# The gates, B and C of each mixer group as 2x2 block products with seven multiplications, and work moved from POOL to ACT

## The chip, the cores and the metric

The kernel runs on one core of one Trainium2 chip. The metric is device time in microseconds (us), the median of several runs. All tensors are float32.

## The reference

A perceiver layer on 8 x 64 = 512 tokens of width 512: cross attention to 8 x 1601 context tokens, then a mixer of the Mamba-2 kind, then a routed low-rank feed-forward. Only the mixer is touched:

```python
proj = jnp.einsum('bld,pd->blp', hidden_states, in_proj_w)   # layernormed x
gate = proj[..., :I]
hbc = proj[..., I:I + CONV_DIM]
dt = proj[..., -H:]
pad = jnp.pad(hbc, ((0, 0), (K - 1, 0), (0, 0)))
conv = conv_bias
for k in range(K):                                            # K = 4 taps
    conv = conv + pad[:, k:k + L, :] * conv_weight[:, k]
xBC = jax.nn.silu(conv)                                       # x, B and C
...                                                           # scan over L = 64 steps
y = y + x * D
yn = y * rsqrt(mean(y * y over the group) + EPS) * norm_weight * silu(gate)
out = jnp.einsum('bli,di->bld', yn, out_proj_w)
```

There are 64 heads of 64 channels, so I = 4096, in 8 groups of 512 channels; each group has a B and a C of 128 channels.

## The kernel before

Cross attention takes the first 2.3 ms and the mixer most of the last 0.5 ms. The Tile framework orders the instructions of each engine's queue from the program order, its own costs and the free buffers; an engine then runs its queue strictly in order. `with tc.issue_after(ins):` adds a constraint to that: instructions of the block that run on the engine of `ins` are queued after `ins`.

The mixer (`mixer_and_routed`) works group by group, channels on partitions, all 512 tokens as columns. A group has ten weight tiles of 512 x 128: n = 0 to 3 the gate, 4 to 7 x, 8 B, 9 C. `project` multiplies one of them with `mx_xnT` in four steps over the width into one PSUM bank with tag `pj` (three of them, shared with `project_out`, whose tile is called `mo`). In the trace each float32 matmul shows as two MATMUL instructions, so a tile is x8. A gate tile goes through Silu on ACT (L1122) into `sg`. An x, B or C tile is convolved on VectorE (DVE): one TENSOR_SCALAR for the first tap and the bias (L1127) and three SCALAR_TENSOR_TENSOR (STT) for the other taps (L1133), all four reading PSUM; then Silu on ACT (L1138) into `xbc`.

The work is pipelined over two groups. In the first half of a group's iteration PE projects tiles 8, 9 and 4 to 7 of group g, with `mix`, `scan` and `gate` of the group before (`old`) between them; GpSimd (POOL) multiplies x by D in `skip` (L1145) into `y`. Then ACT loads the table of Ln and Exp, and takes the decays of the next group (`decay`, L1104 and L1109) and the norm of the old one (`norm`, L1211 to L1215). In the second half PE alternates the four gate tiles with the four `project_out` of the old group (mo0 to mo3); DVE adds each to `x` with the norm's factor `rs` (L1228), which frees its bank. Group 0 has no old group; the last group has no next one and runs its own mix and scan between its gates. After it comes the tail: the last output product and the routed feed-forward.

`load_out` scales the output weights by the norm's weights on POOL (L1015). POOL also forms the decays' inputs `av` (L1089) and adds up the squares (L1196, L1198).

The cross attention's projections already use a 2x2 block product with seven multiplications. The plan and the sums of weights:

```python
FIRST = (("a", "L11", "R11"), ("d", "S2", "T2"), ("b", "S1", "T1"), ("c", "S3", "T3"))
SECOND = (("a", "L12", "R21"), ("b", "S4", "R22"), ("c", "L22", "T4"))
# weight_sums, on POOL: S1 = L21 + L22, S2 = S1 - L11, S3 = L11 - L21, S4 = L12 - S2
```

In the queries' stage (`project_queries`) these products have 256 columns (L204); their results are put together by one ACT copy and five adds on DVE per pair (L220 to L233).

Of the kernel before, what the change touches and what calls it, by code (L numbers as in the profile page):

```python
# [9 lines left out]
F32 = mybir.dt.float32  # L10
AF = mybir.ActivationFunctionType  # L11
# [950 lines left out]
def mixer_and_routed(ctx, tc, c, x, done, w_in, w_out, w_ra, b_w, out):  # L962
# [18 lines left out]
    def bank(tag, shape, name, bufs=1):  # L981
        return (ps4 if tag in ("pj", "y1") else ps).tile(shape, F32, tag=tag, name=name, bufs=bufs)
# [23 lines left out]
    def load_out(G):  # L1006

        g = G.g
        G.wo = wst.tile([P, GC, D], F32, tag="w_out", name=f"w_out_{g}")
        nc.sync.dma_start(  # L1010
            out=G.wo, in_=w_out[g * GC * P : (g + 1) * GC * P, :].rearrange("(n p) o -> p n o", p=P)
        )
        for n in range(GC):
            ct = g * GC + n
            nc.gpsimd.tensor_scalar(G.wo[:, n, :], G.wo[:, n, :], c.nw[:, ct : ct + 1], None, op0=ALU.mult)  # L1015

# [4 lines left out]
    for tt in range(NTT):  # L1021
# [11 lines left out]
    dt = big.tile([P, NTT, H2], F32, name="dt")  # L1033
    z = big.tile([P, NTT, H2], F32, name="sp_z")
    nc.vector.tensor_tensor(z, pdt, c.dtb.unsqueeze(1).to_broadcast([P, NTT, H2]), ALU.add)
    e = big.tile([P, NTT, H2], F32, name="sp_e")

    nc.vector.tensor_scalar(dt, z, 0.0, None, op0=ALU.max)
    nc.vector.scalar_tensor_tensor(out=e, in0=dt, scalar=-2.0, in1=z, op0=ALU.mult, op1=ALU.add)
    nc.scalar.activation(e, e, AF.Exp)  # L1040
    u = big.tile([P, NTT, H2], F32, name="sp_u")
    nc.vector.tensor_scalar(u, e, 1.0, None, op0=ALU.add)
    lu = big.tile([P, NTT, H2], F32, name="sp_lu")
    nc.scalar.activation(lu, u, AF.Ln)
# [9 lines left out]
    nc.scalar.activation(a_sb, c.a_log, AF.Exp)  # L1054
    a = big.tile([P, NTT, H2], F32, name="a")
    nc.vector.scalar_tensor_tensor(
        out=a, in0=dt, scalar=-1.0, in1=a_sb.unsqueeze(1).to_broadcast([P, NTT, H2]),
        op0=ALU.mult, op1=ALU.mult,
    )


# [21 lines left out]
    def steps(G, tt):  # L1083


        if tt == 0:
            G.av, G.dec = [], grpp.tile([P, NTT, HPG, S], F32, tag="dec", name="dec")
        av = wk.tile([P, 2, HH, S], F32, tag="av", name="av", bufs=4)
        nc.gpsimd.tensor_tensor(  # L1089
            av,  # L1090
            ah[:, :, tt, G.g, :].unsqueeze(3).to_broadcast([P, 2, HH, S]),
            c.upto1.unsqueeze(1).unsqueeze(1).to_broadcast([P, 2, HH, S]),
            ALU.mult,
        )
        G.av.append(av)
# [16 lines left out]
    def project(G, n):  # L1112

        pj = bank("pj", [P, NT], "pj", 3)
        for dc in range(DC):
            nc.tensor.matmul(  # L1116
                pj, lhsT=G.w[:, dc, n, :], rhs=xnT[:, dc, :], start=dc == 0, stop=dc == DC - 1
            )
        if n < GC:
            if n == 0:  # L1120
                G.sg = grpp.tile([P, GC, NT], F32, tag="sg", name="sg")
            return nc.scalar.activation(G.sg[:, n, :], pj, AF.Silu).ins  # L1122
        if n == 8:
            G.xbc = grpp.tile([P, GC + 2, NT], F32, tag="xbc", name="xbc")
        ct = G.g * GC + n - GC if n < 8 else (I2 // P + G.g if n == 8 else I2 // P + G2 + G.g)
        acc = wk.tile([P, NT], F32, tag="acc", name="acc", bufs=3)
# [5 lines left out]
        for k in range(1, KC):  # L1132
# [4 lines left out]
            )  # L1137
        return nc.scalar.activation(G.xbc[:, n - GC, :], acc, AF.Silu).ins  # L1138

    def skip(G):  # L1140

        G.y = grpp.tile([P, GC, NT], F32, tag="y", name="y")
        for n in range(GC):
            ct = G.g * GC + n
            nc.gpsimd.tensor_scalar(G.y[:, n, :], G.xbc[:, n, :], c.dk[:, ct : ct + 1], None, op0=ALU.mult)  # L1145

# [74 lines left out]
    def project_out(G, tt):  # L1221
        po = bank("pj", [P, D], "mo", 3)
        for n in range(GC):
            nc.tensor.matmul(  # L1224
                po, lhsT=G.y[:, n, tt * P : (tt + 1) * P], rhs=G.wo[:, n, :],
                start=n == 0, stop=n == GC - 1,
            )
        nc.vector.scalar_tensor_tensor(  # L1228
            out=x[:, tt, :], in0=po, scalar=G.rs[tt], in1=x[:, tt, :], op0=ALU.mult, op1=ALU.add
        )  # L1230


    w = big.tile([P, DC, E + E * R], F32, name="w_ra")
    bw = big.tile([P, D], F32, name="bw")

# [5 lines left out]
    def load_routed():  # L1241
        nc.sync.dma_start(out=w, in_=w_ra.rearrange("(dc p) o -> p dc o", p=P))
        nc.sync.dma_start(out=bw, in_=b_w)

    def route(tt):
        xnT = wk.tile([P, DC, P], F32, tag="xnT", name="rt_xnT")
        layernorm_T(nc, c, small, ps, x, tt, xnT, tag="px", bufs=2, pbufs=1, copy=nc.scalar.copy)
# [13 lines left out]
        nc.vector.tensor_scalar(rw, rank, first, top, op0=ALU.is_equal, op1=ALU.mult)  # L1261
        wh = wk.tile([P, E, R], F32, tag="wh", name="wh")
        nc.vector.tensor_tensor(
# [6 lines left out]
        nc.tensor.transpose(pt, wh.rearrange("p e r -> p (e r)"), c.ident)  # L1270
        whT = wk.tile([P, P], F32, tag="whT", name="whT")
        nc.scalar.copy(whT, pt)
        po = bank("y1", [P, D], "ro")
        nc.tensor.matmul(po, lhsT=whT, rhs=bw, start=True, stop=True)
        o = wk.tile([P, D], F32, tag="o", name="o")
        nc.vector.tensor_tensor(o, x[:, tt, :], po, ALU.add)
        nc.sync.dma_start(out=out[tt * P : (tt + 1) * P, :], in_=o)


    g0 = groups[0]  # L1280
    for tt in range(NTT):
        steps(g0, tt)
    last = None
    for tt in range(NTT):
        last = decay(g0, tt)
    for g in range(G2):
# [10 lines left out]
        with tc.issue_after(last):  # L1297

            for n, behind in (
                (None, ((mix, 0),)),  # L1300
# [6 lines left out]
            ):  # L1307
                if n is not None:
                    silus.append(project(G, n))
                if old:  # L1310
                    for what, tt in behind:
                        what(old, tt)
            skip(G)
        with tc.issue_after(silus[-1]):
            table = load_ln_exp(nc).ins
        with tc.issue_after(table):
            if new:
                decay(new, 0)
                decay(new, 1)
        gates = [lambda n=n: project(G, n) for n in range(GC)]  # L1320
        if new:
# [3 lines left out]
        if old:  # L1325
            with tc.issue_after(table):
                last = norm(old, range(NTT))
        with tc.issue_after(last):
            for n in range(GC):
                if not new and n == NTT - 1:  # L1330
                    scan(G, n)
                    squares(G, n)
                last_gate = gates[n]()
                if not new:

                    for tt in ((0, 1), (2,), (3,), ())[n]:
                        mix(G, tt)
                    if 0 < n < NTT - 1:
                        scan(G, n - 1)
                        squares(G, n - 1)  # L1340
                    if n == 2:
                        scan(G, n)
                        squares(G, n)
                if old:
                    project_out(old, n)
        last = last_gate

    G = groups[-1]
    with tc.issue_after(last):
        table = load_ln_exp(nc).ins  # L1350
# [75 lines left out]
```

## Time and profile before

| | us |
|---|---|
| median of 3 runs (lowest, highest) | 2804.25 (2802.63, 2805.12) |
| the profiled execution | 2806.07 |
| its span, first to last instruction | 2804.4 |
| mixer, first projection to last gate | 2308.2 to 2767.4 |
| groups 1 to 6, from the start of one to the next | 58.8 to 59.6 |

In the profile, PE is TensorE's matmuls, PEld its weight loads, DVE VectorE, ACT ScalarE, POOL GpSimd, and SP the queue that issues DMAs. A line of the timeline has start, duration, engine, source line, operation, output<-inputs, shapes and count; in brackets the engine's idle time before it and what ended it. Matmul ends are modelled, so PE's pace is read from start to start; DVE instructions overlap a little in the same way.

### The profile page before, as it was taken

What the parts mean: (1) busy time and instruction counts of PE and PEld (TensorE: products, weight loads), DVE (VectorE), ACT (ScalarE), POOL (GpSimd) and SP (SyncE); (2) the same over time, 40 slices, a digit from 0 to 9 for tenths busy, and PEclk for the clock granted to TensorE, in tenths of its full rate; (3) what the DMA queues carried; (4) which work ended last, traced back from release to release, by engine and by line L of the source; (5) the groups of instructions that cost most, each with busy time, mean ns of one, the idle gap of its engine ahead of it and who ended that gap; (6) DMA issues with size and microseconds to landing.
All of it is one profiled execution on the core that took longest, in us unless ns stands there. A gap on an engine that the chain in (4) does not pass through costs nothing.

```text
span 2804.4 us, 38363 instructions
## 1 busy us (share of the span) xinstructions
PE 2777.7 (99%) x14972; PEld 1980.5 (71%) x14972; DVE 1717.9 (61%) x3044; ACT 726.3 (26%) x1314; POOL 837.4 (30%) x786
## 2 busy tenths in 40 slices
PE   9899999999999999999999999999999999999998
PEld 7677777777777777877777777778777554444444
DVE  4556676566666666765766676667656326444554
ACT  3322223222222322232222222222322103222222
POOL 4313323322222332233222223322322214333431
PEclk9999999999999999999999999999999999999999
DMA  4821322131223213221311232132212541112200
GB/s 156 276 90 46 88 67 55 53 103 44 48 54 90 54 45 89 67 55 52 103 45 48 54 89 54 48 85 67 61 31 80 168 140 38 53 53 86 72 16 15
DMA packets 277230, 206.02 MB, mean 73 GB/s; under 512 B 155676, under 2 KB 240538, under 8 KB 276026
## 3 DMA queue, kind: packets, MB, share of 16 engines
q1 hardware_dynamic: 277050, 203.57, 25.5%
q8 instruction: 119, 1.95, 0.3%
q14 instruction: 61, 0.50, 0.1%
HBM read 180.87 MB, written 22.66 MB: 73 GB/s over the span
## 4 chain that ended last, share of the span: by engine, by line
PE 87%; DVE 3%; ACT 1%; DMA 1%; issue 0%; POOL 0%; SPq 0%; ACTq 0%; DVEq 0%
PE pav L596 13%; PE psc L526 12%; PE pj L1116 8%; PE pv_a L445 6%; PE pv_b L445 6%; PE pk_b L385 6%; PE pv_c L445 6%; PE pk_c L385 6%; PE pk_a L385 5%; PE mo L1224 4%; PE pv_d L445 3%; PE pk_d L385 3%; PE psn L414 2%; DVE acc L1133 1%; PE pvl L468 1%; PE po_d L741 1%
## 5 line engine op out<-in xcount | busy, mean ns | idle before, releaser
L531 DVE SCALAR_TENSOR_TENSOR attn<-psc,rk,mask_sb 128x256 f32<-128x256 f32 (+1 forms) x832 | 364.4, 475 | 190.6 <-PE psc L526 188.8
L580 POOL TENSOR_TENSOR sm<-attn 128x512 f32<-128x512 f32 x64 | 82.0, 1281 | 1196.0 <-ACT attn L578 1196.0
L596 PE MATMUL pav<-attn,v 128*128 128x256 f32 (+1 forms) x1664 | 384.3, 381 | 0.0
L526 PE MATMUL psc<-q,kT 128*128 128x256 f32 x1536 | 367.5, 380 | 0.0
L596 PEld LDWEIGHTS pav<-attn,v 128*128 128x128 f32 (+1 forms) x1664 | 311.1, 190 | 55.4 <-issue 11.1
L583 POOL TENSOR_TENSOR sm<-sm,attn 128x512 f32<-128x512 f32 x256 | 339.9, 1328 | 28.9 <-DVE attn L574 10.6
L526 PEld LDWEIGHTS psc<-q,kT 128*128 128x128 f32 x1536 | 287.5, 190 | 77.1 <-issue 29.9
L1116 PE MATMUL pj<-mx_xnT,w_in 128*128 128x512 f32 x640 | 296.3, 603 | 1.3 <-DVE acc L1133 1.3
L574 DVE TENSOR_TENSOR attn<-attn,nb 128x1024 f32<-128x1024 f32 x192 | 224.7, 1215 | 58.1 <-ACT nb L571 57.3
L445 PEld LDWEIGHTS pv_a<-wv,cx 128*128 128x128 f32 x1536 | 196.0, 191 | 48.2 <-issue 41.4
L578 ACT ACTIVATE attn<-attn 128x1024 f32<-128x1024 f32 x192 | 203.4, 1059 | 79.8 <-DVE attn L574 77.2
L445 PE MATMUL pv_a<-wv,cx 128*128 128x128 f32 x1536 | 213.8, 279 | 0.0
L542 DVE TENSOR_TENSOR mx<-mx,attn 128x512 f32<-128x512 f32 x256 | 212.3, 829 | 2.0
L1116 PEld LDWEIGHTS pj<-mx_xnT,w_in 128*128 128x128 f32 x640 | 115.2, 190 | 129.4 <-issue 124.7
L385 PE MATMUL pk_a<-cx,wk 128*128 128x417 f32 (+1 forms) x512 | 193.3, 500 | 0.8 <-ACT qrs L110 0.8
L396 ACT ACTIVATE ksq<-kT 128x834 f32<-128x834 f32 (+1 forms) x128 | 109.2, 871 | 145.9 <-DVE kT L377 145.9
L385 PEld LDWEIGHTS pk_a<-cx,wk 128*128 128x128 f32 x512 | 97.2, 190 | 46.1 <-issue 20.8
L1228 DVE SCALAR_TENSOR_TENSOR x<-mo,rs,x 128x512 f32<-128x512 f32 x32 | 24.0, 750 | 165.1 <-PE mo L1224 110.4
L1224 PE MATMUL mo<-w_out,y 128*128 128x512 f32 x256 | 118.1, 597 | 0.0
L643 POOL TENSOR_TENSOR o<-o,f 128x512 f32<-128x512 f32 x31 | 40.0, 1291 | 232.7 <-DMA f<-sums_d 199.3
L571 ACT COPY nb<-nbs 128x256 f32<-128x256 f32 x64 | 24.1, 376 | 318.3 <-DMA nbs<-max_d 309.1
L1133 DVE SCALAR_TENSOR_TENSOR acc<-pj,small_consts,acc 128x504 f32<-128x504 f32 (+1 forms) x144 | 103.7, 724 | 0.7
(220 smaller groups left out, 4187.7 us busy)
## 6 DMA issues: line engine op xcount, KB each, us to landing
wk<-in_wk SPq DMA_DIRECT2D x32, 512.0 KB
wv<-in_wv SPq DMA_DIRECT2D x32, 512.0 KB
w_in<-in_w_in SPq DMA_DIRECT2D x16, 1024.0 KB
wvs<-wv_s_d SPq DMA_DIRECT2D x28, 512.0 KB
wks<-wk_s_d SPq DMA_DIRECT2D x28, 512.0 KB
cx<-in_ctxT SPq DMA_DIRECT2D x16, 834.0 KB
cx<-in_ctxT SPq DMA_DIRECT2D x16, 768.0 KB
wq<-in_wq SPq DMA_DIRECT2D x16, 512.0 KB
```

What stands on the lines that cost most here:

```text
L385: nc.tensor.matmul(ps[:, :w], lhsT=u.wk[l][:, dc, :], rhs=u.cx.r[ch][r][:, dc, :], start=start and dc == 0, stop=dc == 1, skip_group_check ...
L445: nc.tensor.matmul(ps[:, i * HD : (i + 1) * HD], lhsT=u.cx.r[ch][r][:, dc, i * P : (i + 1) * P], rhs=u.wv[l][:, dc, :], start=start and i ...
L526: nc.tensor.matmul(ps[:rows, t - t2, :], lhsT=lhsT, rhs=qh, start=True, stop=True)
L531: nc.vector.scalar_tensor_tensor(out=s.at[:rows, t, :].rearrange("p (h q) -> p h q", h=GQ), in0=ps[:rows, t - t2, :].rearrange("p (h q) -> ...
L542: nc.vector.tensor_tensor(s.mx2, s.mx2, s.at[:, t2 : t2 + 2, :], ALU.max)
L574: nc.vector.tensor_tensor(at[:, k : k + 4, :], at[:, k : k + 4, :], nb.unsqueeze(1).to_broadcast([P, 4, 256]), ALU.add,)
L578: nc.scalar.activation(at[:, k : k + 4, :], at[:, k : k + 4, :], AF.Exp)
L583: nc.gpsimd.tensor_tensor(sm2, sm2, at[:, i : i + 2, :], ALU.add)
L596: nc.tensor.matmul(s.av[:, 0, :], lhsT=u.v[:rows, t, hh, :], rhs=s.at[:rows, t, :], start=t == 0, stop=t == NKT - 1,)
L1116: nc.tensor.matmul(pj, lhsT=G.w[:, dc, n, :], rhs=xnT[:, dc, :], start=dc == 0, stop=dc == DC - 1)
L1133: nc.vector.scalar_tensor_tensor(out=accb[:, :, k:], in0=pjb[:, :, : S - k], scalar=c.cw[:, ct, KC - 1 - k : KC - k], in1=accb[:, :, k:], ...
L1224: nc.tensor.matmul(po, lhsT=G.y[:, n, tt * P : (tt + 1) * P], rhs=G.wo[:, n, :], start=n == 0, stop=n == GC - 1,)
```

## The change

Tiles 8 and 9, 0 and 1, and 2 and 3 of each group are computed as pairs by seven products of 256 x 128 weights with 256 columns. The sums of the weights are made on POOL (`sums_in`, twelve additions a group), those of the tokens once on DVE (`token_sums`). A pair takes two `pj` banks and has two parts, with other work queued between them. B and C are put together in SBUF, their first tap with the bias runs on ACT (Identity), and the other three read SBUF. `skip` and the scaling of the output weights (`weigh_out`) move from POOL to ACT, the fourth skip behind the norm. To make room, `av` has three buffers instead of four, the softplus temporaries (`sp_z`, `sp_e`, `sp_u`, `sp_lu`, `a`) lie in a buffer of `y`, some tiles of the routed part share buffers, and its weights `bw` are loaded after the last group. Tiles 4 to 7 stay as they were. The diff, cut to its core:

```diff
         nc.sync.dma_start(
             out=G.wo, in_=w_out[g * GC * P : (g + 1) * GC * P, :].rearrange("(n p) o -> p n o", p=P)
         )
+    def weigh_out(G):
         for n in range(GC):
-            ct = g * GC + n
-            nc.gpsimd.tensor_scalar(G.wo[:, n, :], G.wo[:, n, :], c.nw[:, ct : ct + 1], None, op0=ALU.mult)
+            ct = G.g * GC + n
+            nc.scalar.activation(G.wo[:, n, :], G.wo[:, n, :], AF.Copy, scale=c.nw[:, ct : ct + 1])
+    def sums_in(G, n):
+        l = {
+            f"L{k + 1}{e + 1}": G.w[:, 2 * e : 2 * e + 2, n + k, :] for k in range(2) for e in range(2)
+        }
+        G.l = getattr(G, "l", {})
+        G.l[n] = weight_sums(nc, l, wk.tile([P, 4, 2, P], F32, tag="ws", name="ws", bufs=3))
     load_in(groups[0])
...
+    HT = NT // 2
+    blocks = {
+        f"R{e + 1}{half + 1}": xnT[:, 2 * e : 2 * e + 2, half * HT : (half + 1) * HT]
+        for e in range(2) for half in range(2)
+    }
+    ts = big.tile([P, 4, 2, HT], F32, name="mx_xs")
+    blocks.update((f"T{k + 1}", ts[:, k]) for k in range(4))
+    def token_sums():
+        for o, p, q in (
+            ("T1", "R12", "R11"), ("T2", "R22", "T1"), ("T3", "R22", "R12"), ("T4", "R21", "T2")
+        ):
+            nc.vector.tensor_tensor(blocks[o], blocks[p], blocks[q], ALU.subtract)
-        av = wk.tile([P, 2, HH, S], F32, tag="av", name="av", bufs=4)
+        av = wk.tile([P, 2, HH, S], F32, tag="av", name="av", bufs=3)
...
         pj = bank("pj", [P, NT], "pj", 3)
         for dc in range(DC):
-            nc.tensor.matmul(
+            done = nc.tensor.matmul(
                 pj, lhsT=G.w[:, dc, n, :], rhs=xnT[:, dc, :], start=dc == 0, stop=dc == DC - 1
-            )
-        if n < GC:
-            if n == 0:
-                G.sg = grpp.tile([P, GC, NT], F32, tag="sg", name="sg")
-            return nc.scalar.activation(G.sg[:, n, :], pj, AF.Silu).ins
-        if n == 8:
-            G.xbc = grpp.tile([P, GC + 2, NT], F32, tag="xbc", name="xbc")
-        ct = G.g * GC + n - GC if n < 8 else (I2 // P + G.g if n == 8 else I2 // P + G2 + G.g)
+            ).ins
+        ct = G.g * GC + n - GC
...
-        return nc.scalar.activation(G.xbc[:, n - GC, :], acc, AF.Silu).ins
-
-    def skip(G):
-
-        G.y = grpp.tile([P, GC, NT], F32, tag="y", name="y")
-        for n in range(GC):
+        return done, nc.scalar.activation(G.xbc[:, n - GC, :], acc, AF.Silu).ins
+    def project_pair(G, n):
+        st, l = Group(), G.l[n]
+        if n == 0:
+            G.sg = grpp.tile([P, GC, NT], F32, tag="sg", name="sg")
+        if n == 8:
+            G.xbc = grpp.tile([P, GC + 2, NT], F32, tag="xbc", name="xbc")
+        to = G.sg[:, n : n + 2] if n < 8 else G.xbc[:, GC :]
+        def product(k, lhs, rhs, start, stop):
+            for dc in range(2):
+                last = nc.tensor.matmul(
+                    st.ps[k], lhsT=l[lhs][:, dc, :], rhs=blocks[rhs][:, dc, :],
+                    start=start and dc == 0, stop=stop and dc == 1, skip_group_check=True,
+                ).ins
+            return last
+        def first():
+            st.ps = {}
+            for pair in ("ab", "cd"):
+                t = bank("pj", [P, 2, HT], f"pj_{pair}", 3)
+                st.ps[pair[0]], st.ps[pair[1]] = t[:, 0, :], t[:, 1, :]
+            for k, lhs, rhs in FIRST:
+                last = product(k, lhs, rhs, k in "ad", False)
+            p1 = wk.tile([P, HT], F32, tag="p1", name="p1", bufs=1)
+            nc.scalar.copy(p1, st.ps["a"])
+            st.u2 = wk.tile([P, HT], F32, tag="u2", name="u2", bufs=1)
+            nc.vector.tensor_tensor(st.u2, p1, st.ps["d"], ALU.add)
+            nc.vector.tensor_tensor(p1, st.u2, st.ps["b"], ALU.add)
+            nc.vector.tensor_tensor(to[:, 1, HT:], p1, st.ps["c"], ALU.add)
+            return last
+        def second():
+            for k, lhs, rhs in SECOND:
+                last = product(k, lhs, rhs, False, True)
+            nc.scalar.activation(to[:, 0, :HT], st.ps["a"], AF.Silu if n < 8 else AF.Copy)
+            nc.vector.tensor_tensor(to[:, 0, HT:], st.u2, st.ps["b"], ALU.add)
+            nc.vector.tensor_tensor(to[:, 1, :HT], st.u2, st.ps["c"], ALU.add)
+            if n == 8:
+                for k in range(2):
+                    ct = I2 // P + k * G2 + G.g
+                    acc = wk.tile([P, NT], F32, tag="acc", name="acc", bufs=3)
+                    nc.scalar.activation(
+                        acc, to[:, k], AF.Identity, bias=c.cb[:, ct : ct + 1], scale=c.cw[:, ct, KC - 1 : KC]
+                    )
+                    accb = acc.rearrange("p (b t) -> p b t", b=B)
+                    tob = to[:, k].rearrange("p (b t) -> p b t", b=B)
+                    for j in range(1, KC):
+                        nc.vector.scalar_tensor_tensor(
+                            out=accb[:, :, j:], in0=tob[:, :, : S - j],
+                            scalar=c.cw[:, ct, KC - 1 - j : KC - j], in1=accb[:, :, j:],
+                            op0=ALU.mult, op1=ALU.add,
+                        )
+                    silu = nc.scalar.activation(to[:, k], acc, AF.Silu).ins
+                return last, silu
+            nc.scalar.activation(to[:, 0, HT:], to[:, 0, HT:], AF.Silu)
+            return last, nc.scalar.activation(to[:, 1, :], to[:, 1, :], AF.Silu).ins
+        return first, second
+    def skip(G, ns):
+        if ns[0] == 0:
+            G.y = grpp.tile([P, GC, NT], F32, tag="y", name="y")
+        for n in ns:
             ct = G.g * GC + n
-            nc.gpsimd.tensor_scalar(G.y[:, n, :], G.xbc[:, n, :], c.dk[:, ct : ct + 1], None, op0=ALU.mult)
+            nc.scalar.activation(G.y[:, n, :], G.xbc[:, n, :], AF.Copy, scale=c.dk[:, ct : ct + 1])
...
+    sums_in(groups[0], 8)
+    token_sums()
     g0 = groups[0]
     for tt in range(NTT):
         steps(g0, tt)
-    last = None
+    last = done_out = None
     for tt in range(NTT):
         last = decay(g0, tt)
     for g in range(G2):
         silus = []
         with tc.issue_after(last):
+            both = project_pair(G, 8)
             for n, behind in (
                 (None, ((mix, 0),)),
                 (8, ((mix, 1),)),
                 (6, ((gate, 1), (scan, 3))),
                 (7, ((gate, 2), (gate, 3))),
             ):
-                if n is not None:
-                    silus.append(project(G, n))
+                if n == 8:
+                    done = both[0]()
+                elif n == 9:
+                    with tc.issue_after(done):
+                        done, silu = both[1]()
+                elif n is not None:
+                    done, silu = project(G, n)
+                if n is not None and n != 8:
+                    silus.append(silu)
                 if old:
-                    for what, tt in behind:
-                        what(old, tt)
-            skip(G)
+                    with tc.issue_after(done if n is not None else done_out):
+                        for what, tt in behind:
+                            what(old, tt)
+            skip(G, range(GC - 1))
+        if g == 0:
+            sums_in(G, 0)
+            sums_in(G, 2)
         with tc.issue_after(silus[-1]):
             table = load_ln_exp(nc).ins
         with tc.issue_after(table):
             if new:
                 decay(new, 0)
                 decay(new, 1)
-        gates = [lambda n=n: project(G, n) for n in range(GC)]
         if new:
             with tc.issue_after(table):
                 last2 = decay(new, 2)
         if old:
             with tc.issue_after(table):
                 last = norm(old, range(NTT))
+        def own(*what):
+            if not new:
+                for step, tt in what:
+                    step(G, tt)
         with tc.issue_after(last):
-            for n in range(GC):
-                if not new and n == NTT - 1:
-                    scan(G, n)
-                    squares(G, n)
-                last_gate = gates[n]()
-                if not new:
-
-                    for tt in ((0, 1), (2,), (3,), ())[n]:
-                        mix(G, tt)
-                    if 0 < n < NTT - 1:
-                        scan(G, n - 1)
-                        squares(G, n - 1)
-                    if n == 2:
-                        scan(G, n)
-                        squares(G, n)
-                if old:
-                    project_out(old, n)
+            skip(G, [GC - 1])
+        done_out = None
+        for k in range(2):
+            first, second = project_pair(G, 2 * k)
+            if k:
+                own((scan, 3), (squares, 3))
+            with tc.issue_after(done_out) if k else nullcontext():
+                done_out = first()
+            if not k:
+                own((mix, 0), (mix, 1))
+            if old:
+                with tc.issue_after(done_out):
+                    done_out = project_out(old, 2 * k)
+            if not k:
+                own((scan, 0), (squares, 0), (mix, 2))
+            with tc.issue_after(done_out), tc.issue_after(last):
+                done_out, last_gate = second()
+            if not k:
+                own((scan, 1), (squares, 1), (mix, 3))
+            if old:
+                with tc.issue_after(done_out):
+                    done_out = project_out(old, 2 * k + 1)
+            if not k:
+                own((scan, 2), (squares, 2))
+            if new and k:
+                for n in (8, 0, 2):
+                    sums_in(new, n)
+        with tc.issue_after(last_gate):
+            weigh_out(G)
         last = last_gate
+    bw = wk.tile([P, HPG, PD], F32, tag="dx", name="bw").rearrange("p h d -> p (h d)")
+    nc.sync.dma_start(out=bw, in_=b_w)
```

More of the change, by code (lines that the diff above doesn't have):

```diff
@@ L1033, in mixer_and_routed @@
     dt = big.tile([P, NTT, H2], F32, name="dt")
-    z = big.tile([P, NTT, H2], F32, name="sp_z")
+    sp = grpp.tile([P, GC, NT], F32, tag="y", name="sp")
+    z, e, u, lu = (
+        sp[:, k, : NTT * H2].rearrange("p (t h) -> p t h", h=H2) for k in range(4)
+    )
     nc.vector.tensor_tensor(z, pdt, c.dtb.unsqueeze(1).to_broadcast([P, NTT, H2]), ALU.add)
-    e = big.tile([P, NTT, H2], F32, name="sp_e")
     nc.vector.tensor_scalar(dt, z, 0.0, None, op0=ALU.max)
@@ L1040, in mixer_and_routed @@
     nc.scalar.activation(e, e, AF.Exp)
-    u = big.tile([P, NTT, H2], F32, name="sp_u")
     nc.vector.tensor_scalar(u, e, 1.0, None, op0=ALU.add)
-    lu = big.tile([P, NTT, H2], F32, name="sp_lu")
     nc.scalar.activation(lu, u, AF.Ln)
@@ L1054, in mixer_and_routed @@
     nc.scalar.activation(a_sb, c.a_log, AF.Exp)
-    a = big.tile([P, NTT, H2], F32, name="a")
+    a = sp[:, 0, NTT * H2 :].rearrange("p (t h) -> p t h", h=H2)
     nc.vector.scalar_tensor_tensor(
@@ L1137, in project @@
             )
-        return nc.scalar.activation(G.xbc[:, n - GC, :], acc, AF.Silu).ins
-    def skip(G):
-        G.y = grpp.tile([P, GC, NT], F32, tag="y", name="y")
-        for n in range(GC):
+        return done, nc.scalar.activation(G.xbc[:, n - GC, :], acc, AF.Silu).ins
[47 more added lines that the diff above has]
+                            op0=ALU.mult, op1=ALU.add,
+                        )
+                    silu = nc.scalar.activation(to[:, k], acc, AF.Silu).ins
[3 more added lines that the diff above has]
+        return first, second
@@ L1223, in project_out @@
         for n in range(GC):
-            nc.tensor.matmul(
+            last = nc.tensor.matmul(
                 po, lhsT=G.y[:, n, tt * P : (tt + 1) * P], rhs=G.wo[:, n, :],
@@ L1230, in project_out @@
         )
+        return last.ins
     w = big.tile([P, DC, E + E * R], F32, name="w_ra")
-    bw = big.tile([P, D], F32, name="bw")
     rank = big.tile([P, E], F32, name="rank")
@@ L1242, in load_routed @@
         nc.sync.dma_start(out=w, in_=w_ra.rearrange("(dc p) o -> p dc o", p=P))
-        nc.sync.dma_start(out=bw, in_=b_w)
     def route(tt):
-        xnT = wk.tile([P, DC, P], F32, tag="xnT", name="rt_xnT")
+        xnT = wk.tile([P, DC, P], F32, tag="sq", name="rt_xnT")
         layernorm_T(nc, c, small, ps, x, tt, xnT, tag="px", bufs=2, pbufs=1, copy=nc.scalar.copy)
@@ L1261, in route @@
         nc.vector.tensor_scalar(rw, rank, first, top, op0=ALU.is_equal, op1=ALU.mult)
-        wh = wk.tile([P, E, R], F32, tag="wh", name="wh")
+        wh = wk.tile([P, E, R], F32, tag="wh", name="wh", bufs=1)
         nc.vector.tensor_tensor(
@@ L1270, in route @@
         nc.tensor.transpose(pt, wh.rearrange("p e r -> p (e r)"), c.ident)
-        whT = wk.tile([P, P], F32, tag="whT", name="whT")
+        whT = wk.tile([P, P], F32, tag="whT", name="whT", bufs=1)
         nc.scalar.copy(whT, pt)
@@ L1274, in route @@
         nc.tensor.matmul(po, lhsT=whT, rhs=bw, start=True, stop=True)
-        o = wk.tile([P, D], F32, tag="o", name="o")
+        o = wk.tile([P, D], F32, tag="acc", name="o", bufs=3)
         nc.vector.tensor_tensor(o, x[:, tt, :], po, ALU.add)
         nc.sync.dma_start(out=out[tt * P : (tt + 1) * P, :], in_=o)
+    sums_in(groups[0], 8)
+    token_sums()
     g0 = groups[0]
```

## The prediction

> **What bounds the kernel now.** I read the page's busy times first, then the stretches of the mixer, then the chain of waits through one of its groups, then the timeline at its joints.
>
> ```profile
> PE 2777.7 (99%) x14972; PEld 1980.5 (71%) x14972; DVE 1717.9 (61%) x3044; ACT 726.3 (26%) x1314; POOL 837.4 (30%) x786
> ```
>
> TensorE (PE) is busy for 99% of the span, so time can be won by giving it less. The stretches (busy us of PE, PEld, DVE, ACT, POOL) say the same of a middle group and of group 0:
>
> ```profile
> 2308.00:2351.00 43.00, 41.71 (x152) 16.54 (x152) 22.55 (x39) 15.61 (x32) 18.46 (x16) 1.00 0.00 1
> ...
> 2411.00:2470.00 59.00, 58.79 (x312) 27.00 (x312) 31.11 (x52) 14.25 (x26) 23.21 (x20) 1.00 0.18 60
> ```
>
> DVE has 31 of 59 us, which looks like room. The chain through that group says otherwise (start, us, what):
>
> ```profile
> 2411.84 3.43 PE pj L1116 x8
> ...
> 2425.29 3.65 PE pj L1116 x8
> 2428.96 0.81 DVE acc L1127
> ...
> 2439.25 1.46 DVE y L1205
> ...
> 2442.16 0.74 DVE acc L1133
> 2442.92 0.63 ACT xbc L1138
> 2443.57 1.28 ACT L116
> ...
> 2453.19 3.43 PE mo L1224 x8
> ```
>
> One projected tile takes PE 3.43 us. From 2428.96 to 2442.92 the chain is DVE alone: in the first half of a group DVE runs without a break and ends 4.6 us behind the last projection. Then come Silu, a table load, the decays and the norm, 9.0 us to rs. The timeline shows what waits for that, and one collision:
>
> ```profile
> 2439.17 1.53 DVE L1205 TENSOR_TENSOR y<-y,sg 128x512 f32<-128x512 f32 x1
> 2440.13 2.00 POOL L1145 TENSOR_SCALAR y<-xbc,small_consts 128x512 f32<-128x512 f32 x1
> ...
> 2451.93 0.75 DVE L1228 SCALAR_TENSOR_TENSOR x<-mo,rs,x 128x512 f32<-128x512 f32 x1 [9.05 <-ACT rs L1215]
> 2453.03 2.31 PE L1224 MATMUL mo<-w_out,y 128*128 128x512 f32 x5
> ```
>
> PE's second output product (mo1) needs a pj bank, which x frees once rs is there. Today PE fills the wait with gate 0, mo0 and gate 1 and loses about 0.4 us: PE and the DVE-to-ACT chain are nearly level. After mo1 PE runs alone to the end of the group.
>
> **Matmuls.** The query stage has this block product in this form (seven products, 128x256):
>
> ```profile
> 65.39 1.03 PE L204 MATMUL pq_ab<-xs,wqs 128*128 128x256 f32 x4
> ...
> 66.26 1.03 PE L204 MATMUL pq_cd<-xs,wqs 128*128 128x256 f32 x4
> ```
>
> A product of four instructions starts every 0.86 us, weight loads (0.19 us each) hidden. A pair is 7 x 0.86 = 6.02 us for 2 x 3.43 = 6.86: 0.84 us less, three pairs a group 2.5, 24 pairs 20.2 us. That is all the change can win on PE.
>
> **DVE and ACT, groups 1 to 6.** Removed from DVE: two TENSOR_SCALARs (0.72 us from start to start). Added: five adds a pair (0.42 us, rows L222 to L233 of the query stage). The gates' ten lie where DVE waits 6.12 us before each x. The six further taps of B and C stay, but read SBUF; I price them by their PSUM rows at 0.65 us from start to start (q_st, STT from SBUF, lasts 0.77 against 0.73). From the first matmul of pair 8 (before: 2411.84): first part 3.44 us, mix 1 0.86, second part 2.58, so 6.9; ACT copy 0.37, two adds, Identity 0.63 as Silu of that size: the taps of B and C begin near 8.0, where tile 8's began at 3.5. From there DVE has 6 x 0.65 = 3.9, four tiles at 0.72 + 3 x 0.65 = 10.7, two mixes of 1.4, eight scan adds of 0.33 = 2.6, four gates of 0.60 = 2.4: 22.4 us, ending at 30.4. Before it ended at 2442.92 - 2411.84 = 31.1: 0.7 earlier, because the 0.86 us lost by the gate (1.46 for 0.60) beside POOL's skip is gone with that skip. If as much is lost to other POOL work, it ends 0.2 later.
>
> Then mo1. Its chain is 30.4 + 9.0 + 1.1 (rs to PE's start, as before) = 40.5; before 41.2. PE itself: projection 7 ends at 26.5 - 0.84 = 25.7; first part of pair 0 3.44 and one decay 0.6 to 29.7. That pair now holds two of three pj banks, so mo0 takes projection 7's and waits for DVE until 30.4; then mo0 3.43, decays and norm 2.8, second part 2.58 and 0.8 of switching give 40.0. So mo1 starts at 40.5, 0.7 earlier, although PE had 1.7 less to do; only the pair behind mo1 counts in full. Gain 0.7 + 0.84 = 1.5 us a group; bounds 0.84 less 0.2 and 2.5. Six groups: -9.0.
>
> A rule that speaks against this: by the Trainium skill, "SBUF — State Buffer", summary of rules, a DVE instruction with two SBUF inputs and a GpSimd one that reads SBUF block each other until the first has finished. The gate above (1.53 us, its median 0.68) fits. Six taps a group join that class; were each held for one 0.73 us POOL add, the chain would be 4.4 us longer and the change slower.
>
> **POOL and ACT.** POOL loses skip (four of 1.77 us) and the scaling of w_out (four of 1.57), and gets twelve weight sums of 0.73. ACT gets four skips and four scalings of 0.63, and per pair a copy (0.37): some 8 us, on 14.3 of 59. Three skips lie in DVE's long stretch; the fourth is queued behind the norm, ahead of Silu's table, and delays the gates' Silu, whose bank mo1 does not need. The scaling is queued behind the last gate, ahead of pair 8's copy, which is due 7 us later. Cover gone, each costs its 2.5 us. With av at three buffers the fourth av waits for the first decay, which PE runs at 2438.31, well before the others. I take these at nothing. No row shows Copy or Identity under Silu's table; L134's copy runs between Ln and Exp without a load; if it needed one, 1.28 us twice a group would stand ahead of B's and C's taps. The skill's "ScalarE: Activation LUTs", table sets, has both functions in every set, which no run here shows.
>
> **Group 0.** Pair 8's copy on ACT is queued behind the last decay of group 0:
>
> ```profile
> 2327.69 0.66 ACT L1109 ACTIVATE dec<-seg 128x256 f32<-128x256 f32 x2 [0.99 <-PE seg L1104]
> ...
> 2335.12 6.28 PE L1116 MATMUL pj<-mx_xnT,w_in 128*128 128x512 f32 x14 [1.29 <-DVE acc L1133]
> ```
>
> So from 2311.7 to about 2329.8 the pair keeps two banks, and projections 4, 5, 6 go through the third one at a time, each with its convolution (2.7 us) behind it. PE has 3.44 + 3 x 3.43 + 3.3 (psw, decays) = 17 us of work for 21.6: 4.6 idle where it had none. Against that the pairs' 2.5 us, of which the early one is lost in the idle time, and part of the 1.29. DVE's four token sums (0.65 to 1.21, as L197) come in before the first decay too. I take +2.5; bounds -2.5 and +7.
>
> **Last group and tail.** Saved 2.5; DVE, busy for 41 of 60 us there, gets 4.7 more. I take -1.5, bounds -2.5 and +1.5. In the tail the last scaling (2.5 us of ACT) lies between Silu (2768.17) and the table; rs would come 0.5 later, while x waits for PE until 2775.40. Loading bw late has 20 us to land. Zero, up to +1.3.
>
> Sum: -9.0 + 2.5 - 1.5 = -8.0 us. The profiled execution took 2806.07 (span 2804.4 and 1.7 around it), so 2798.1; the median of the runs lies 1.8 below it, so 2796.2.
>
> **Rivals.** *Everything counts*: the planner keeps PE fed, the chain is short: -20, 2784. For it: PE is 99% busy; against: DVE's unbroken stretch. *Only the pair behind mo1 counts*: six times 0.84, +2.5, -0.8: -3, 2801, no measurable change. For it: POOL's weight sums fall into that stretch, as the skips did. *The chain grows* (slower): each further DVE instruction held by POOL as the gate was adds 0.86 us ahead of rs. Two a group eat the 1.5; three make -8 + 15.5 = +7.5, 2812; six make +23. For it: thirteen two-SBUF-input instructions a group lie there (six taps, three m, four gates), and POOL's sums and squares beside them; against: in before only one or two of seven such were held.
>
> **How the numbers follow.** 0.2%, 5.6 us, is what a measurement of this kernel can tell from no change. Forecast 0.36, everything 0.14, so faster 0.50; the pair alone 0.21; chain grows 0.29. The range from 2786 to 2814 leaves out about 0.07 below and 0.12 above; the forecast's own is 2790 to 2799.
>
> **What would show it.** Right: PE starts a 128x256 product every 0.86 us; taps of B and C at 0.65 to 0.75 us; DVE's last tap 30 to 31 us after pair 8's first matmul; PE idle before mo0 (0.7, DVE) and mo1 (0.5, x); some 4 us idle in group 0; middle groups near 57.9 us for 59.4. Wrong: DVE's last tap beyond 32 us, taps at 1.3 us, or a PE wait on ACT in the gates.

## The result, and the profile after

The changed kernel takes 2823.45 us (median of 4 runs, 2820.97 to 2823.69) against 2804.2 us (4 runs): the ratio is 1.0065, with a 95% interval of 1.0053 to 1.0077. It is slower by 0.65%. I had said 2796.2, faster.

The profiled execution has a span of 2821.8 us, 17.5 more than before. The line of busy times of its page:

```profile
PE 2771.3 (98%) x15260; PEld 2039.0 (72%) x15260; DVE 1758.6 (62%) x3152; ACT 793.1 (28%) x1442; POOL 805.0 (29%) x818
```

TensorE is busy for less (2771 for 2778 us), and the span is longer all the same: it waits more. To see where, I cut the mixer at the same marks in both traces. Times count from the end of the last pdt product, the last matmul ahead of the mixer's own, because runs reach that point up to 4 us apart. "T0" is the first matmul of a group's tile or pair 8, "D7" the end of DVE's last tap.

| part | before | after | difference |
|---|---|---|---|
| pdt to T0 of group 2 (group 0, and group 1's middle part) | 103.30 | 115.76 | +12.46 |
| each group from there to T0 of group 7 (mean of 5) | 59.28 | 60.46 | +1.18 |
| T0 of group 7 to the end | 96.29 | 95.46 | -0.83 |

The first row holds one middle part, 1.18, so group 0 itself lost 11.3 us; six middle parts lost 7.1; the end gained 0.8. Sum +17.5.

**A middle group.** The chain of waits through one (start, us, what):

```profile
2545.00 0.87 PE pj_ab L1173 x4
2545.87 0.86 PE pj_cd L1173 x4
...
2549.31 0.86 PE pj L1142 x2
2550.17 1.74 PE pj_ab L1173 x8
2551.93 0.39 ACT xbc L1198
2552.35 0.43 DVE xbc L1199
2552.81 0.82 ACT acc L1205
2553.65 1.02 DVE acc L1211
2554.67 0.33 DVE y L1273
2555.00 3.67 DVE acc L1211 x4
...
2574.15 0.94 DVE y L1289
...
2576.91 0.41 DVE u L1190
2577.31 0.65 DVE acc L1153
2578.01 2.84 PE mo L1308 x6
...
2587.16 0.76 DVE x L1312
2587.96 2.41 PE mo L1308 x5
```

The products run at 0.86 us as reckoned. From 2553.65 to the last tap the chain is DVE, but it begins at T0 + 8.8 and ends at T0 + 33.1 (before 31.2), and TensorE stands idle for 1.68 us ahead of mo0, which it did not before (0.2 us idle in a whole group):

```profile
2578.01 2.84 PE L1308 MATMUL mo<-w_out,y 128*128 128x512 f32 x6 [1.68 <-DVE acc L1153]
```

While B's and C's taps run, POOL forms pair 8's weight sums for the next group (its timeline: start, us, line, shapes, idle before):

```profile
2553.41 0.73 POOL L141 TENSOR_TENSOR ws<-w_in 128x256 f32<-128x256 f32 x1 [10.56 <-PE py L1267]
2554.09 1.17 POOL L143 TENSOR_TENSOR ws<-w_in 128x256 f32<-128x256 f32 x1
2555.22 1.16 POOL L142 TENSOR_TENSOR ws<-ws,w_in 128x256 f32<-128x256 f32 x1
2556.46 1.04 POOL L144 TENSOR_TENSOR ws<-w_in,ws 128x256 f32<-128x256 f32 x1
```

A sum of this shape takes 0.73 us where DVE leaves it alone and up to 1.17 beside the taps, and the four taps of the one row take 3.67 us, 0.92 each for 0.65. Later in the group POOL's sums of squares meet the third gate on DVE, which takes 1.03 us; the first two gates take 0.68 and 0.69:

```profile
2573.81 0.73 POOL L1280 TENSOR_TENSOR sq<-sq 128x256 f32<-128x256 f32 x1
2574.06 1.03 DVE L1289 TENSOR_TENSOR y<-y,sg 128x512 f32<-128x512 f32 x1
2574.62 0.78 POOL L1282 TENSOR_TENSOR s<-sq 128x128 f32<-128x128 f32 x1
```

**Group 0.** The timeline of TensorE and ACT:

```profile
2311.33 3.60 PE L1142 MATMUL pj<-mx_xnT,w_in 128*128 128x512 f32 x8
2316.91 0.69 PE L1091 MATMUL psw<-sp,ident 128*64 128x256 f32 x4 [1.98 <-DVE sp L1067]
...
2326.23 0.66 ACT L1135 ACTIVATE dec<-seg 128x256 f32<-128x256 f32 x2 [1.22 <-PE seg L1130]
2326.77 0.38 ACT L1188 COPY p<-pj_ab 128x256 f32<-128x256 f32 x1
...
2328.20 2.05 PE L1173 MATMUL pj_ab<-mx_xnT,w_in 128*128 128x256 f32 x4
...
2332.50 7.13 PE L1142 MATMUL pj<-mx_xnT,w_in 128*128 128x512 f32 x16
```

Pair 8's copy (L1188) does come behind the last decay, but one projection, not three, goes through the free bank; the others stand behind pair 8's second part in TensorE's order. And the pair's product at 2328.20 lasts 2.05 us; the same row lasts 1.03 in every middle group. The stretches show why (length, then busy us of PE, PEld, DVE, ACT, POOL, then TensorE's granted clock):

```profile
2313.99:2317.40 3.41, 1.43 (x7) 0.31 (x5) 3.17 (x7) 0.00 (x0) 0.00 (x0) 1.00 0.00 0
2317.40:2331.05 13.65, 9.50 (x49) 4.77 (x48) 1.26 (x3) 3.42 (x11) 8.21 (x8) 0.50 0.01 2
```

After a stretch of 3.41 us in which TensorE was busy for 1.43, its clock was halved for 13.65 us. In before the mixer runs at full clock throughout.

### The profile page after: what moved, and what is told of

Its sections match the earlier page's. It is cut to its first block, busy times and chain, and to the rows that moved or that the text cites. A ratio compares the mean times of both kernels' runs of the same rounds, so it can differ in the third digit from the quotient of the medians.

```text
span 2821.8 us, 39282 instructions
## 1 busy us (share of the span) xinstructions
PE 2771.3 (98%) x15260; PEld 2039.0 (72%) x15260; DVE 1758.6 (62%) x3152; ACT 793.1 (28%) x1442; POOL 805.0 (29%) x818
## 4 chain that ended last, share of the span: by engine, by line
PE 80%; DVE 7%; DMA 1%; ACT 1%; issue 0%; SPq 0%; POOL 0%; ACTq 0%; DVEq 0%
PE pav L596 12%; PE psc L526 12%; PE pv_a L445 6%; PE pv_b L445 6%; PE pk_b L385 5%; PE pv_c L445 5%; PE pk_c L385 5%; PE pk_a L385 5%; PE mo L1308 4%; PE pv_d L445 3%; PE pj_ab L1173 3%; PE pk_d L385 3%; DVE acc L1153 2%; PE psn L414 2%; PE pj_cd L1173 1%; DVE acc L1211 1%
## 5 line engine op out<-in xcount | busy, mean ns | idle before, releaser
L1142 PE MATMUL pj<-mx_xnT,w_in 128*128 128x512 f32 x256 | 122.7, 610 | 1.3 <-DVE acc L1153 1.3
L375 ACT COPY kT<-pk_a 128x384 f32<-128x384 f32 x64 | 31.5, 492 | 266.3 <-PE pk_a L385 266.3
L419 ACT COPY kss<-psn 128x384 f32<-128x384 f32 x64 | 31.5, 493 | 252.7 <-PE psn L414 252.7
L385 PE MATMUL pk_b<-cx,wks 128*128 128x384 f32 (+1 forms) x256 | 97.2, 502 | 1.5 <-DVE t L361 1.5
```

What stands on the lines that cost most here:

```text
L385: nc.tensor.matmul(ps[:, :w], lhsT=u.wk[l][:, dc, :], rhs=u.cx.r[ch][r][:, dc, :], start=start and dc == 0, stop=dc == 1, skip_group_check ...
L1142: done = nc.tensor.matmul(pj, lhsT=G.w[:, dc, n, :], rhs=xnT[:, dc, :], start=dc == 0, stop=dc == DC - 1).ins
```

## Experiments

Theory A: a middle group is D7 + 10.0 us to the second output product + 17.3 us behind it, so only what ends DVE's last tap earlier helps; group 0 is a loss of its own, from the copy's place in ACT's order. Theory B, the rival: TensorE is slowed by the block products themselves, and DVE's end is hidden. Each of the first four runs takes one suspect away; before is 2805.07 us there.

**1. Pair 8's copy not behind group 0's decays.** In group 0, both parts of pair 8 are no longer ordered behind the decays, only its Silu is.

```diff
-        with tc.issue_after(last):
-            both = project_pair(G, 8)
+        both = project_pair(G, 8)
...
-                    done = both[0]()
+                with tc.issue_after(last) if g else nullcontext():
+                    done = both[0]()
```

> Edit: in group 0 alone, the ACT instructions of pair 8 except its two Silus are no longer queued behind the group's last decay. Theory A (group 0's loss of about 11 us is pair 8's copy waiting on ACT behind the decays, two pj banks held meanwhile, and the half clock that follows PE's idle time): first projection to first matmul of group 1 falls from 55 us to within 2 us of the 44 us of before, the half clock near 2317 us is gone, and the total falls by 9 to 12 us, to 2812 to 2815. Rival: the loss is DVE's token sums ahead of softplus, or the two banks as such; then under 3 us comes back. Middle groups stay at 60.4 us by both.

Measured: 2814.38 us, ratio 1.0031 (1.0018 to 1.0044). Pdt to T0 of group 2 is 108.45 instead of 115.76; the half clock of group 0 is gone; the middle groups stay at 60.4. One stretch at half clock (3.41 us, ahead of group 1's mo1) is new and costs 1.6 of it (D7 to mo1 11.65 instead of 10.01). So the copy's place is worth 7.3 us, 8.9 without that stretch, of group 0's 11.3.

**2. Gates as pairs, B and C as before.** Tiles 8 and 9 go through `project` again, and pair 8's sums are left out.

```diff
-                if n == 8:
-                    done = both[0]()
-                elif n == 9:
-                    with tc.issue_after(done):
-                        done, silu = both[1]()
-                elif n is not None:
+                if n is not None:
                     done, silu = project(G, n)
...
-                for n in (8, 0, 2):
+                for n in (0, 2):
```

> Edit: B and C projected and convolved from PSUM as before; only the gates are pairs; everything else of the change stays. Theory B (a middle group's length is DVE's last tap plus 10 us to mo1 plus 17.3 us, whatever PE has to do before): the last tap comes 30.5 to 31.5 us after the group's first matmul instead of 33.1, a middle group takes 58 to 58.8 us instead of 60.4 although PE gets 0.84 us more, and group 0 falls back to about 43 us: in all 2823 - 12 - 11 = 2800, with 4 us either way. Rival (PE's work sets the group): a group gets 0.84 us longer, 61.3, and only group 0 is won back: about 2817.

Measured: 2800.53, ratio 0.9984 (0.9975 to 0.9993): faster than before. D7 at T0 + 31.1, mo1 10.03 later, T0 of the next group 17.3 behind that; a group is 58.46. Everything that the change lost came with pair 8.

**3. Pair 8's weight sums behind POOL's squares.**

```diff
-                for n in (8, 0, 2):
+                with tc.issue_after(old.squared) if old else nullcontext():
+                    sums_in(new, 8)
+                for n in (0, 2):
                     sums_in(new, n)
```

> Edit: the four weight sums of the next group's B and C are queued on POOL behind the last squares of the old group, so they no longer run beside B's and C's taps; nothing else moves. Theory B with the lock: the six taps go back from 0.88 to about 0.65 us from start to start, the last tap comes 1.3 us earlier, a middle group takes 59.1 us, the total falls by 6 to 9 us to 2815 to 2817. Rival (the taps are slow because they read SBUF, or the chain has its length elsewhere): taps keep 0.9 us, or the groups keep 60.4 us; total within 2 us of the change.

Measured: 2817.93, ratio 1.0045 (1.0030 to 1.0060). DVE's timeline of a middle group, the same two pieces as in the chain above:

```profile
2549.62 0.74 DVE L1211 SCALAR_TENSOR_TENSOR acc<-xbc,small_consts,acc 128x504 f32<-128x504 f32 x1 [0.43 <-ACT acc L1205]
...
2550.61 2.67 DVE L1211 SCALAR_TENSOR_TENSOR acc<-xbc,small_consts,acc 128x496 f32<-128x496 f32 x4
...
2566.59 0.42 DVE L1273 TENSOR_TENSOR y<-y,py 128x256 f32<-128x256 f32 x1 [0.50 <-PE py L1267]
```

Four taps take 2.67 us instead of 3.7, so 0.65 each: the price that I had put in, once POOL is quiet. D7 comes 0.9 earlier (T0 + 32.2) and not 1.35, since DVE then waits 0.5 for TensorE (last line). A group is 59.51.

**4. Gates 2 and 3, and pair 0's adds, behind DVE's last tap.**

```diff
-            nc.vector.scalar_tensor_tensor(
+            G.convolved = nc.vector.scalar_tensor_tensor(
...
+        after = groups[G.g + 1].convolved if tt > 1 else None
+        with tc.issue_after(after) if after else nullcontext():
+            nc.vector.tensor_tensor(G.y[:, :, tok], G.y[:, :, tok], G.sg[:, :, tok], ALU.mult)
...
-            with tc.issue_after(done_out) if k else nullcontext():
+            with tc.issue_after(done_out) if k else tc.issue_after(G.convolved):
```

> Edit: the old group's last two gate multiplications and the first add of pair 0 are queued on DVE behind the last tap; the work is the same. Theory B: the last tap comes 1.5 to 2 us earlier, mo0 and mo1 with it, a middle group takes 58.6 to 59 us, the total falls by 8 to 11 us to 2813 to 2815. Rival (PE or ACT bounds the way to mo1 close behind DVE): the last tap comes earlier, but mo1 by less than 0.6 us; the total falls by less than 4 us.

Measured: 2813.15, ratio 1.0027 (1.0017 to 1.0038). DVE's timeline at the end of its stretch:

```profile
2569.70 2.27 DVE L1153 SCALAR_TENSOR_TENSOR acc<-pj,small_consts,acc 128x504 f32<-128x504 f32 x3
2571.89 1.28 DVE L1291 TENSOR_TENSOR y<-y,sg 128x512 f32<-128x512 f32 x2
2573.09 0.41 DVE L1190 TENSOR_TENSOR u<-p,pj_cd 128x256 f32<-128x256 f32 x1
```

The last three taps follow each other with nothing between; D7 is at T0 + 31.6 instead of 33.1, mo1 again 10.01 later, a group 59.03.

In these four D7 lies between 31.1 and 33.1 us behind T0, while D7 to mo1 (10.0) and mo1 to the next T0 (17.3) stay, but for a stretch at half clock. That is theory A. The next four runs (before: 2804.6 us) put the mends together, take the control, and test a step of mine that had not come up.

**5. The three mends of 1, 3 and 4 in one kernel.**

> The change with three things moved together: pair 8's copy of group 0 no longer queued behind the decays, pair 8's weight sums behind POOL's squares, and gates 2 and 3 with pair 0's adds behind DVE's last tap. Theory A (DVE's stretch up to the last tap, plus a constant 10.0 to the second output product and 17.3 behind it, sets the group; group 0 stands apart): the last tap 30.6 to 30.8 us after pair 8's first matmul (33.1 less 0.9 for the sums and 1.5 for the gates), a middle group 58.0, T0 of group 2 near 2414; six groups at 2.4 less than the change and some 8 less in group 0, so 2797 to 2800 us, below the kernel before by 0.1 to 0.3%. Theory B (PE's own count of matmuls sets the group, DVE's end is hidden): no sum of the three, 2808 or above. If the parts only overlap (each gives back the same DVE time), 2805 or above.

Measured: 2799.91, ratio 0.9985 (0.9976 to 0.9993); D7 at T0 + 30.84, a group 58.16, pdt to T0 of group 2 106.17. The gains add up but for a small rest (0.34, 0.20 and 0.38% alone, 0.92 in sum; 0.80% together). My 30.4 for D7 and 57.9 for a group were near what this order gives, not what the change's order gives.

**6. Gates as pairs (as in 2) and the late gates (as in 4).**

> Only the gates are block products, B and C are projected as in the kernel before, and gates 2 and 3 of the group before and pair 0's adds stand behind DVE's last tap. Theory A: the last tap 29.6 to 30.0 us after the first matmul of tile 8 (31.1 with gate pairs alone, less 1.5), second output product 10.0 later, a group of 57.0 to 57.4 us, against 58.45 with the gates in the old place; 2790 to 2794 us, ratio 0.995 to 0.996. At that length PE's own work (59.2 less 1.7 for two pairs, 57.5) is about level with the chain, so the gain of the order can be cut at 57.5, then 2794 to 2796. Theory B (PE alone): no gain over the gate pairs in the old order, 2800.

Measured: 2793.53, ratio 0.9958 (0.9945 to 0.9970). **7. The kernel before, with only the late gates of 4:**

> The kernel before with its gates 2 and 3 behind DVE's last tap, nothing else. Theory A: DVE's last tap comes 1.2 to 1.5 us earlier, but PE lost only about 0.4 us a group there, so a group falls by 0.2 to 0.5 us at the most: 2801 to 2804. If the order alone were what the mends above win, it would be 2796 or less, and the block products would be worth nothing.

Measured: 2802.46, ratio 0.9993 (0.9984 to 1.0003), not to be told from no change. A middle group of each in its stretches, 5 first, then 6, then 7:

```profile
2528.02:2586.18 58.16, 57.75 (x350) 34.10 (x349) 35.11 (x66) 22.75 (x42) 18.43 (x24) 1.00 0.19 64
```

```profile
2527.16:2584.34 57.18, 57.18 (x338) 31.39 (x337) 34.50 (x63) 20.37 (x38) 15.46 (x20) 1.00 0.19 66
```

```profile
2529.75:2588.67 58.92, 58.92 (x314) 26.91 (x313) 30.55 (x53) 14.36 (x26) 22.76 (x20) 1.00 0.19 63
```

In 6 and 7 TensorE is busy for the whole group, so their difference is its work alone: 58.92 - 57.18 = 1.74 us for two pairs, against the 2 x 0.84 of the prediction. In 5 there are three pairs, and the group is 0.98 us longer than with two. TensorE is not busy for less there either: 57.75 us against 57.18, so the 0.84 us that the third pair was to save is not to be seen. How much of the 57.75 is waiting inside what counts as busy, these rows can't say.

**8. Skip and the scaling of w_out back on POOL.**

```diff
-            nc.scalar.activation(G.wo[:, n, :], G.wo[:, n, :], AF.Copy, scale=c.nw[:, ct : ct + 1])
+            nc.gpsimd.tensor_scalar(G.wo[:, n, :], G.wo[:, n, :], c.nw[:, ct : ct + 1], None, op0=ALU.mult)
...
-            nc.scalar.activation(G.y[:, n, :], G.xbc[:, n, :], AF.Copy, scale=c.dk[:, ct : ct + 1])
+            nc.gpsimd.tensor_scalar(G.y[:, n, :], G.xbc[:, n, :], c.dk[:, ct : ct + 1], None, op0=ALU.mult)
```

> The change with skip and the scaling of w_out back on POOL, as before it. My step that put ACT's eight further us at nothing: if right, ACT's relief gives nothing back, and POOL's four skips of 1.8 us again meet a gate on DVE (1.5 us for 0.7), so DVE's last tap comes 33 to 34.5 us after pair 8's first matmul and a middle group takes 60.2 to 61.5: 2822 to 2830. If ACT's load was on the path instead (skip ahead of Silu's table, scaling ahead of pair 8's copy), a group falls by 0.5 or more and the time goes below 2820.

Measured: 2824.95, ratio 1.0074 (1.0061 to 1.0088), no better than the change. Three of five groups took 60.24 to 60.90; two took 62.4 and 62.6, with 3.41 us at half clock in each. Nothing came back when ACT got its old load. D7 to mo1 stays at 10.0 us (11.7 in the two groups with half clock), so ACT's further work was not on that way. Ahead of D7 the run is less clear, since POOL's longer queue takes its own price there: in one group two gates take 0.89 and 0.94 us and an m 1.08, for 0.68 each, and D7 is near T0 + 33.4. But in the chain of the change ACT has, ahead of D7, only the copy and the Identity that I had counted.

These two groups and their neighbours gave a measure of the clock. Stretches of one of the groups that fell, and of one that didn't:

```profile
2573.12:2576.53 3.41, 1.46 (x7) 0.98 (x6) 3.40 (x6) 0.67 (x2) 1.80 (x2) 1.00 0.02 5
2576.53:2579.94 3.41, 3.41 (x5) 1.37 (x5) 0.42 (x1) 2.27 (x4) 1.56 (x1) 0.50 0.00 0
2634.55:2637.96 3.41, 1.69 (x8) 1.14 (x6) 3.41 (x6) 0.37 (x1) 2.31 (x2) 1.00 0.00 0
2637.96:2641.37 3.41, 3.18 (x14) 1.27 (x14) 0.93 (x3) 2.57 (x4) 1.56 (x1) 1.00 0.00 0
```

3.41 - 1.46 = 1.95 us idle is followed by half clock, 3.41 - 1.69 = 1.72 is not. The records of half clock within a run lie whole multiples of 3.41 us apart. On that grid, in the mixers of the change and of runs 1 to 6 and 8, all eleven falls followed a stretch with 1.95 to 2.76 us idle, none followed one with 1.72 or less, and no stretch at full clock lay between. The last two runs (before: 2805.31 us) test this as a cause.

**9. TensorE kept busy in group 0 of the change** with products that nobody reads: 8 behind the first projection, 6 behind psw, 3 behind each of the four decays: 26, not the 29 of the expectation. The views show each product as two matmuls.

```diff
+    def warm(n, after, idle):
+        with tc.issue_after(after):
+            for _ in range(n):
+                nc.tensor.matmul(idle, lhsT=c.ones, rhs=c.ones, start=True, stop=True)
...
+    warm(6, shifted, idle[0])
...
         last = decay(g0, tt)
+        warm(3, g0.seg, idle[0])
...
+                if g == 0 and n == 4:
+                    with tc.high_priority(offset=tc.tile_snap_priority() - early):
+                        warm(8, done, idle[1])
```

> The change with 29 small products on TensorE in group 0's waits (128x128, 0.21 us each, into two idle banks; nobody reads them): eight behind the first projection, six behind psw, three behind each decay. Theory C (the clock falls to half because TensorE stands idle for more than about 1.9 us of a stretch of 3.41 us; the traces so far have it fall after stretches with 1.95 to 2.76 us idle and never after 1.72 or less): no stretch at half clock in group 0; decays follow each other at 1.65 us instead of 1.87 (4 x 0.22), pair 8's second part takes 2.6 instead of 4.3 us, so pair 8 of group 2 starts 2.5 to 3 us earlier than in the change (2424.1), at 2421 to 2421.6, and the time is 2819.5 to 2821.5; the other 8 us of group 0 stay, they are the copy's place behind the decays. Rival D (the clock has another cause): half clock for 13.65 us as before, 2823 or more. Rival E (all of group 0's loss is the clock): 2813 to 2815.

Measured: 2818.27, ratio 1.0048 (1.0035 to 1.0062), 1.2 us below the range that I gave; the profiled execution, 2820.51, lies in it. The two stretches in which the change fell to half clock:

```profile
2313.99:2317.40 3.41, 3.22 (x27) 2.64 (x26) 2.36 (x7) 0.52 (x2) 0.00 (x0) 1.00 0.00 0
2317.40:2331.05 13.65, 12.80 (x90) 8.25 (x90) 4.21 (x8) 4.80 (x12) 11.27 (x12) 1.00 0.01 2
```

The clock stayed whole. From pdt to group 1's mo0 it is 85.1 us instead of 88.5, so the half clock had cost 3.4 us. At T0 of group 2 only 1.7 of them are left, since a stretch at half clock (3.41 us after 2.12 idle) fell ahead of mo1 in group 1. So group 0's loss of 11.3 us is 3.4 of clock, some 5.5 of waiting that ends with the copy (8.9 less 3.4), and a rest of 2.4 that stays in run 1. There TensorE waits 2.41 us for a convolution before pair 0 has its two banks; in before it waits 1.29 us for one in group 0. That this wait is the rest is a guess: no run takes it out of the change. Run 1's timeline:

```profile
2335.16 1.13 PE L1173 MATMUL pj_ab<-mx_xnT,w_in 128*128 128x256 f32 x4 [2.41 <-DVE acc L1153]
```

**10. The same with nine products in the one long wait of group 0 of kernel 6.**

```diff
+                if g == 0 and n == 7:
+                    warm(9, done)
```

> The kernel with gate pairs alone and the late gates, and nine such small products (1.9 us) in the one long wait of group 0 (3.27 us, for DVE's convolutions, behind projection 7). Theory C: 1.4 us of that wait are left, the 6.83 us at half clock go, pair 0's first part takes 3.44 instead of 6.7 us, and tile 8 of group 2 starts at 2409.6 to 2411 instead of 2412.8; 2790 to 2792 us, ratio 0.9950 to 0.9955; the middle groups stay at 57.18. Rival D: no difference, 2793.5.

Measured: 2791.99, ratio 0.9955 (0.9942 to 0.9969). TensorE's timeline at that wait (3.27 us in kernel 6):

```profile
2329.61 2.17 PE L990 MATMUL idle<-ones 128*128 128x128 f32 x18
2331.72 0.66 PE L1135 MATMUL seg<-av,past 64*64 64x256 f32 x8
2333.64 1.13 PE L1180 MATMUL pj_ab<-mx_xnT,w_in 128*128 128x256 f32 x4 [1.26 <-DVE acc L1160]
```

The 6.83 us at half clock are gone, pair 0's products run at their rate (1.13 for 2.07), and pdt to T0 of group 2 falls from 106.02 to 102.98. The trace shows these 3.0 us; the medians (1.5 lower, overlapping intervals) can't. This kernel has the lowest median of those here, and it is faster than before and the change.

## Why the prediction was wrong, point by point

Of the 25.5 us between my -8.0 and the profile's +17.5, 16.1 lie in the six middle groups (-9.0 reckoned, +7.1 measured), 8.8 in group 0 (+2.5, +11.3), 0.7 in the last group and tail (-1.5, -0.8).

**The step that failed first: D7 at 30.4 us.** It was 33.1. The terms, from the trace:

- *The start of B's and C's taps*, 8.0 reckoned, 8.8 measured. Two matmuls of projection 4 (0.86 us, in the chain above) come between pair 8's parts, where I had counted mix 1 alone. Against that, ACT's copy starts behind two products of the second part and not behind all three, so it comes at T0 + 7.1, for 6.9 reckoned. From there the chain has the copy, one add and the Identity, 1.7 us in all. My "near 8.0" left 1.1 for them; my own prices (0.37, 0.42 and 0.63) make it 1.4, which is 8.3.
- *Six taps at 0.65*: 0.874 from start to start, +1.35. I had the risk, two SBUF inputs beside POOL, and put it into the rival instead of the sum; run 3 shows that POOL's sums are the cause, since the taps fall to 0.65 without them.
- *Pair 0's first add* ahead of the last tap, +0.41, though I counted the gates' ten adds as lying in waits; run 4 moves it out.
- *The gate beside POOL*: one of four took 1.03 instead of 0.68, +0.35. The skips had gone from POOL; the squares had not, and the gate lies beside them (the rows above).

Sum 2.9, for 2.7 measured. In before TensorE was full, so DVE's end had stood just short of being the bound; the 1.7 us that the pairs were to take off TensorE ahead of mo1 could count for nothing once DVE's end came later.

**Group 0: +2.5 reckoned, +11.3 measured.** The queue that I named was the right one (run 1), the size was not. I let three projections through the third bank; TensorE's order held one. Runs 1 and 9 put what ends with the copy's place at 8.9 us, some 5.5 of waiting and 3.4 of clock. For the clock I had no term: my own 4.6 us idle should have been asked what they do to TensorE's rate. What the last 2.4 of the 11.3 are stays open.

**The rival that came true** is "the chain grows", the slower one: its mechanism, DVE held by POOL, was there, at 0.22 us a tap rather than 0.86, with a gate besides; the price for three such (+7.5, 2812) and for six (+23, 2827) enclosed the 2823 that was measured. That they do is in part luck: POOL's part is 1.35 + 0.35 = 1.7 of the 2.7 us by which DVE's end was late; the start and the add are no part of it, and 11.3 of the 17.5 us are group 0's.

By the Trainium skill, "SBUF — State Buffer", summary of rules, the later of the two instructions waits for the whole of the earlier. The rows show less: 0.22 us a tap, and 0.3 to 0.45 us a sum, against the 0.73 that a full wait for a sum would have cost, and both sides pay.

**What held.** A product in 0.86 us, 0.84 us saved a pair for the gates (1.74 for two, runs 6 and 7); for pair 8 no run shows it. D7 to mo1 in 10.1 (10.0). The part behind mo1 shorter by 0.84 (18.02 to 17.3, so 0.72). ACT's further work at nothing behind D7 (run 8), and ACT's timeline has no table load ahead of a middle group's Copy and Identity. So the forecast's balance was right, and the sign hung on D7 and on group 0.

## What to carry to other kernels

Where an engine is nearly full because another's chain ends just as it is needed, price the change on that chain first: here three pairs were to save 2.5 us of TensorE a group. The two that left DVE's chain alone won 0.16% in the old order and 0.42% once DVE's late work stood behind its last tap, while the third, which starts the convolutions 5.3 us later (T0 + 8.8 for 3.5), cost more than it saved. An engine's idle time at a joint is not only its own length: look for the stretches of 3.4 us that are more than half empty, since the work behind them may run at half rate, as it did here twelve times. And put a risk that a row already shows (a gate of 1.53 us for 0.68) into the sum at a middle price rather than into a rival alone.

## What the runs showed of the hardware that was not expected

In the mixers TensorE's clock fell to half after each stretch of 3.41 us in which it was idle for 1.95 us or more, and after none with 1.72 or less (twelve falls, in the mixers of nine kernels). It came back in steps of 3.41 us, after 3.41 to 13.65 us. One such stretch with TensorE busy should cost half of it, 1.7 us; run 1 shows 1.6 and run 10 3.0 for two. The edge is less sharp outside the mixers: in the cross attention of run 9 half clock followed a stretch with 1.69 us idle (109.84 to 113.25) and did not follow one with 1.95 (85.94 to 89.35). So 1.72 and 1.95 bound what these mixers show and are no threshold. The Trainium skill, "TensorE: Matmul & The Clock Gate", Part 1, speaks of a free-running window of about 3.4 us and of half rate after an idle one; the grid agrees, but no window here had to be idle as a whole: 57% (1.95 of 3.41 us) was enough in the mixers.

A DVE instruction with two SBUF inputs and POOL's additions slow each other in part: the tap takes 0.87 us for 0.65, the sum 1.04 to 1.17 for 0.73. A tap that reads PSUM kept its 0.73 us (start 2565.52) beside POOL's sum of squares (2565.64), which kept its 0.73 too.
